# Graph attention and a four-layer end stage: written places for each bank job and reader, the clamp on VectorE, and an end stage issued in written order

## The chip, the core and the metric

The kernel runs on one core of a Trainium2 chip. The metric is the device time in microseconds (us) of one execution. A core has TensorE (matmuls; PE in the profile, its weight loads PEld), VectorE (DVE), ScalarE (ACT), GpSimd (POOL) and SyncE (SP, which here issues most DMAs). TensorE writes to PSUM, which has eight banks; all other tiles lie in SBUF. A matmul of 32-bit floats appears as two matmul instructions in the trace.

## What is computed

Four graph layers follow each other; x has 16 batches of 1024 nodes with 128 features, adj is a sparse 1024 x 1024 matrix per batch.

```python
x = _layernorm(x + L0(x, adj))            # attention
x = _layernorm(x + L1(x, adj, nodemask))  # neighbours thinned out one row after the other, three SAGE layers with batch norm
x = _layernorm(x + L2(x, adj))
x = _layernorm(x + L3(x, adj))

def L0(h, adjacency):
    h_self = h @ W_self_w + W_self_b; h_nb = h @ W_nb_w + W_nb_b
    pre = (h_self @ A1_i)[:, :, None, :] + (h_nb @ A1_j)[:, None, :, :] + A1_b
    scores = (relu(pre) @ A2_w)[..., 0] + A2_b[0]
    attn = softmax(where(adjacency == 0, -1e9, scores))
    return relu(h_self + attn @ h_nb)

def L2(x, adj):
    return relu(adj @ (x @ W + b) + x)

def L3(H, A):
    A1 = A + eye; d = rsqrt(sum(A1, -1))
    return (A1 * d[:, :, None] * d[:, None, :]) @ H @ B
```

## The kernel before

The kernel has one stage after the other. The change touches two of them: the attention (`phase_att`, layer 0) and the end stage (`phase_end`, the last product of layer 1 with its layernorm, then layers 2 and 3).

**Attention.** Since adj is sparse, scores are computed for edges, not for pairs of nodes. The nodes of a batch are cut into 10 groups of 104. A pair of groups (i, j) with j >= i is a unit; a unit holds up to 128 edges, one per partition. Eleven units form a block (`band(r)`), five blocks a batch, so that a batch has 55 units, called slots in the order of the work, and the stage 880. For each unit, `gather` (L516, L521) multiplies the one-hot tables of the edges' ends with the projected features, into one of three PSUM banks `pg`; `score` (VectorE, L533) and `weigh` (ScalarE, L543 and L545) make the weights `hg`; `scatter` (L554) adds the weighted features into three PSUM banks `pa` that hold the batch's sums. The scatter of a unit follows three slots later.

The one-hot tables of a block are made while earlier blocks run, in small jobs on TensorE: `counts` and `offsets` (number the edges of each unit, L351, L362), `beyond` on GpSimd (L374 subtracts, L378 clamps to 0..1; tile `g`, one buffer), `steps` (L411, the difference of clamped rows gives the one-hot table `oh_b` of one end), `ranks` (L383, L389, tile `qs`), `others` (L427; VectorE L435 compares) and `numbers` (L447); `widen` (ScalarE, L441) makes 32-bit copies `oh`, `numbered` (VectorE, L501) the table `we` for the scatter, `one_way` (VectorE, L403) a test for edges without their counterpart. Each job takes one of two PSUM banks `pw` and is followed by its readers on ScalarE or VectorE. The projection of a group of the next batch (`projection`, L303, L306) takes such a bank too; three readers on ScalarE (L315 to L317) and three instructions on VectorE (L318 to L321) follow. Of the batch before, `collect` (L565) takes the sums out of `pa`, `clear` (L264) zeroes them, `end_group` (L598 to L79) finishes a group and its statistics, `end_norm` (L619) the layernorm, `end_turn` (L635, L639) transposes. The mask rows of a later batch are loaded by SP and converted by GpSimd (L280, L282).

The loop `for at in range(B * SLOTS)` writes all of this slot by slot: the gather, then the matmuls of the slot's jobs, the score, the readers of the jobs, the weights, the scatter. `block_job` decides the job of a slot: `steps` in slots 0 to 2 of a block, `others` in 3 to 5, projections in 6 and 7, `ranks` with `counts`, `offsets` and `numbers` in 8 to 10. `as_traced` chains the instructions of each engine, so that every engine runs them in the order in which they are written.

**End stage.** For each batch b, `layer2` and `layer3` run eight iterations each: `neighbours` (L1647, 8 products of adj with `vals` or `v`), then on VectorE the residual sum and the statistics of the rows (`stats`, L78, L79). After iterations 3 and 7, `root` raises the variances of four row tiles to -1/2 on GpSimd (L1586, L1587); `apply` (VectorE, L1591) normalizes them, `turn` transposes them (L1619; ScalarE copies, L1620), `values_2` and `values_3` make the next layer's values (L1626). In between, the next batch's `products_1` (L1603), `rows_1` (the sum with x, L1608, its statistics and the root) and `bias_1` (GpSimd, L1575) are written. `store_slots` issues two indirect DMAs from GpSimd (L1521) that put rows of batch b + 4 into `x1_d`; it is done for b up to 11. `negative` (ScalarE, L1706) tests adj. There is no `as_traced` here: the order on each engine is chosen by the framework's scheduler from priorities and its own estimates.

## Time and profile before

| | |
|---|---|
| Median of 3 runs | 3051.52 us (3046.65 to 3052.65) |
| Profiled execution | 3058.9 us, of which the span from the first to the last instruction is 3056.8 |
| Mean granted TensorE clock | 0.937 |
| Attention stage | from the first score at 59 us to about 1600 us |
| End stage, first product of layer 2 to the end | 2359.75 to 3056.8 us |

The profile is of one execution, taken by the hardware profiler. Durations of matmuls are modelled at their ends, so that TensorE's busy time is not its peak. "Idle before" and the waits are inferred from semaphores. In the views of windows a row has the window, its length, then the busy time of PE, PEld, DVE, ACT and POOL (with the number of instructions), then the mean granted TensorE clock, the share of the DMA engines and GB/s. In the view of waits a row has the waiting instruction, the one that it waits for, the sum in us, the number of waits and the longest. In the timeline and in the chain of waits, the first two numbers are start and length in us.

### The profile page before, as it was taken

The numbers are of one execution on the slowest core, as the hardware profiler recorded it, in microseconds if no ns is written. First come the engines' busy times: TensorE is split into PE (matmuls) and PEld (weight loads), VectorE is DVE, ScalarE is ACT, GpSimd is POOL, SyncE is SP. The second block draws the span as 40 slices with busy tenths as digits, with TensorE's granted clock in tenths as the row PEclk, the third lists the DMA queues.
The fourth block names the chain that finished last, engine by engine and source line by source line (L and its number), as shares of the span: only waits on it lengthen the run. The fifth ranks groups of instructions, "written<-read, shape, count | busy, mean of one in ns | idle before, by whom it ended". The sixth has DMA issues, their size and how long they took to land.

```text
span 3056.8 us, 70983 instructions
## 1 busy us (share of the span) xinstructions
PE 2723.7 (89%) x25724; PEld 2392.3 (78%) x25724; DVE 2191.9 (72%) x8416; ACT 1860.8 (61%) x5689; POOL 1426.8 (47%) x1545
## 2 busy tenths in 40 slices
PE   5999999999999999999968888578796999999997
PEld 3877777777777777777768887377786999999997
DVE  5788888888888888888863567756664666666664
ACT  3888888888888888888862233255654233343332
POOL 3766665666666666666313331244333333233321
PEclk8999999999999999999987777789997999999999
DMA  5323332233322333223026442054455354445440
GB/s 145 100 73 96 102 95 81 71 99 98 93 79 75 103 98 93 76 73 97 22 58 210 145 150 60 17 178 160 169 193 192 113 181 161 147 146 181 160 152 16
DMA packets 179958, 348.60 MB, mean 114 GB/s; under 512 B 14148, under 2 KB 89942, under 8 KB 179472
## 3 DMA queue, kind: packets, MB, share of 16 engines
q1 hardware_dynamic: 173584, 328.15, 33.7%
q0 software_dynamic: 4864, 11.63, 1.3%
q10 hardware_dynamic: 1152, 4.19, 0.5%
q8 instruction: 206, 3.38, 0.5%
q14 instruction: 152, 1.25, 0.1%
HBM read 257.87 MB, written 87.03 MB: 113 GB/s over the span
## 4 chain that ended last, share of the span: by engine, by line
PE 46%; DVE 28%; ACT 9%; issue 7%; DMA 6%; POOL 3%; SPq 0%; POOLq 0%; ACTq 0%; DVEq 0%
PE pg L1647 10%; PE pa L554 5%; DVE junk L533 5%; PE pg L516 4%; PE pg L521 3%; PE pq L1357 3%; DVE we L501 2%; DMA x_d<-keep_xs,keep_row 2%; ACT hg L545 2%; DVE oh_b L435 2%; DVE one_way L403 2%; PE pg L1007 2%; ACT oh L441 2%; DVE st L78 2%; DVE x_rows L601 2%
## 5 line engine op out<-in xcount | busy, mean ns | idle before, releaser
L545 ACT ACTIVATE hg<-pg,hg 128x128 f32<-128x128 f32 x1600 | 510.2, 365 | 28.6
L554 PE MATMUL pa<-hg,we 128*104 128x129 f32 (+1 forms) x3520 | 526.1, 272 | 0.0
L516 PE MATMUL pg<-parts,oh 104*128 104x384 f32 (+1 forms) x1760 | 512.8, 373 | 3.5 <-ACT hg L545 3.3
L554 PEld LDWEIGHTS pa<-hg,we 128*104 128x104 f32 x3520 | 447.7, 171 | 46.5 <-issue 38.2
L533 DVE SCALAR_TENSOR_TENSOR junk<-pg,w_a 128x128 bf16<-128x128 f32 x1600 | 396.7, 281 | 110.9 <-PE pg L521 104.4
L280 POOL TENSOR_SCALAR mask<-ld 104x1024 f16<-104x1024 f32 (+1 forms) x150 | 426.5, 2843 | 39.6 <-DMA ld<-in_adjT 39.4
L521 PE MATMUL pg<-parts,oh 104*128 104x384 f32 (+1 forms) x1760 | 434.3, 328 | 0.0
L374 POOL TENSOR_TENSOR g<-k_next,off 105x512 f16<-105x512 f16 (+1 forms) x240 | 236.4, 985 | 366.4 <-PE pw L411 360.9
L521 PEld LDWEIGHTS pg<-parts,oh 104*128 104x128 f32 x1760 | 311.4, 189 | 0.0
L543 ACT ACTIVATE hg<-sc 128x2 f32<-128x2 f32 (+1 forms) x880 | 187.8, 213 | 160.8 <-DVE junk L533 147.4
L516 PEld LDWEIGHTS pg<-parts,oh 104*128 104x128 f32 x1760 | 268.8, 191 | 21.5 <-ACT oh L441 15.1
L501 DVE TENSOR_TENSOR we<-k_id,ids 128x832 f32<-128x832 f16 (+1 forms) x240 | 259.2, 1080 | 9.3 <-PE pa L554 8.7
L1587 POOL TENSOR_TENSOR rstd<-ve,mhalf 128x4 f32<-128x4 f32 x96 | 97.0, 1011 | 323.9 <-DVE ve L1586 323.8
L441 ACT CAST oh<-oh_b 104x1024 fp32r<-104x1024 bf16 (+1 forms) x240 | 233.4, 973 | 1.0 <-DVE oh_b L435 1.0
L378 POOL TENSOR_SCALAR g<-g 105x512 f16<-105x512 f16 (+1 forms) x240 | 188.7, 786 | 20.7
L303 PE MATMUL pw<-w_all,xT 128*104 128x512 f32 x320 | 172.1, 620 | 24.7 <-ACT x1T L639 9.4
L318 DVE TENSOR_TENSOR parts<-pw,parts 104x384 fp32r<-104x384 f32 x160 | 88.9, 556 | 123.2 <-ACT own L317 122.0
L1591 DVE TENSOR_SCALAR x<-x,mv,rstd 128x128 f32<-128x128 f32 x256 | 104.7, 450 | 91.2 <-POOL rstd L1587 91.2
L435 DVE TENSOR_TENSOR oh_b<-pw,k_slot_edge 104x512 bf16<-104x512 f32 (+1 forms) x240 | 152.6, 636 | 5.6 <-PE pw L427 5.6
L1696 ACT ACTIVATE y<-x,shift,rstd 128x128 f32<-128x128 f32 x128 | 52.7, 482 | 162.9 <-POOL shift L1689 162.9
L403 DVE SCALAR_TENSOR_TENSOR one_way<-qs,mask 104x1040 bf16<-104x1040 f16 (+9 forms) x160 | 146.7, 917 | 1.1 <-ACT qs L396 1.1
L420 ACT CAST oh_b<-pw 104x512 bf16<-104x512 f32 (+1 forms) x240 | 131.2, 547 | 20.4 <-PE pw L411 20.0
(349 smaller groups left out, 6522.1 us busy)
## 6 DMA issues: line engine op xcount, KB each, us to landing
ld<-in_adjT SPq DMA_DIRECT2D x135, 416.0 KB
m<-mask_d SPq DMA_DIRECT2D x16, 2048.0 KB
keep_adj<-in_adjT SPq DMA_DIRECT2D x8, 4096.0 KB
adj<-in_adjT SPq DMA_DIRECT2D x8, 4096.0 KB
mask_d<-mask SPq DMA_DIRECT2D x144, 208.0 KB
hT_d<-uT SPq DMA_DIRECT2D x48, 512.0 KB
h<-hT_d SPq DMA_DIRECT2D x48, 512.0 KB
hT<-hT_d SPq DMA_DIRECT2D x32, 512.0 KB
```

The costliest lines, as they stand in the source:

```text
L280: engine.tensor_scalar(mt[:n, s, :N], ld[:n], 0.0, None, op0=ALU.is_gt)
L374: nc.gpsimd.tensor_tensor(g, k_next[:E].unsqueeze(1).to_broadcast([E, m, C]), v.off[:, n0 : n0 + m].unsqueeze(2).to_broadcast([E, m, C]), ...
L403: nc.vector.scalar_tensor_tensor(junk[:W, :nb, :], v.q[:W, at : at + nb, :W], EDGE, v.mt[:W, i, i * W : NP].rearrange("p (n w) -> p n w", ...
L435: nc.vector.tensor_tensor(v.o[:W, n0 : n0 + m, 1, :], pw[:W, : m * C].rearrange("p (n c) -> p n c", c=C), k_slot_edge[:W].unsqueeze(1).to_ ...
L441: nc.scalar.copy(v.ends[:W, n0 : n0 + m], v.o[:W, n0 : n0 + m])
L501: nc.vector.tensor_tensor(we[:, :n, :], k_id.unsqueeze(1).to_broadcast([P, n, W]), V[b * BANDS + r].ids[:, 2 * lo : 2 * hi].unsqueeze(2).t ...
L516: nc.tensor.matmul(flat[:, first : 3 * F], own, d.parts[i][:W, p, first:], start=p == 0, stop=False, skip_group_check=True,)
L521: nc.tensor.matmul(pg[:, 1::step, :], other, reversed_parts(d.parts[j][:W, p, :], step), start=False, stop=p == 1, skip_group_check=True,)
L533: nc.vector.scalar_tensor_tensor(junk, pg[:, 1 + e, :], 0.0, w_a2, op0=ALU.max, op1=ALU.mult, accum_out=d.sc[:, at + e : at + e + 1],)
L545: nc.scalar.activation(hg[:, e, :F], pg[:, 3 - 3 * e, :], AF.Copy, scale=hg[:, e, F : F + 1])
L554: nc.tensor.matmul(PA[bank][:W, at : at + part.stop - part.start], we[:, 2 * (u - lo) + e, :], hg[:, e, part], start=False, stop=True, ski ...
L1647: nc.tensor.matmul(pg[:, :cols], ADJ[b % 2][:, jt, it * P : (it + 1) * P], v[:, jt, :cols], start=jt == 0, stop=jt == T - 1,)
```

## The change

In attention the slot loop and `block_job` go. Every step gets a written place, a number of slots and a fraction, and all steps are issued in the order of these places: `BANKS` has the place of each bank job within a block, `READ` that of each of its readers, `PROJECT` those of the two projections of a block (the products, then each of the six readers), and so on. The readers of a projection become single steps. The clamp of `beyond` moves from GpSimd to VectorE (`clamp`) and has its own places. The first three blocks' tables, written out by hand before, come from the same table, ahead of slot 0. The masks of batch 1 come every two slots instead of every three; those of later batches get places of their own (`MASKS`).

In the end stage `rows_1` is split into the sum (`add_1`) and the statistics (`stats_1`), with a PSUM tile for each half; transposes and the sum over neighbours run over their parts in reversed order; several steps change places, the two indirect stores among them (from layer 2 to iterations 3 and 5 of layer 3); and `as_traced` fixes the written order on each engine.

The diff, cut:

```diff
+BANKS = (
+    (-2.05, (("step", 0),)), (-0.7, (("step", 1),)), (1.5, (("step", 2),)), (2.05, (("other", 0),)),
+    (3.1, (("other", 1),)), (4.42, (("rank", 1),)), (5.5, (("rank", 0), ("count", 0),)), (5.58, (("other", 2),)),
+    (6.38, (("rank", 2), ("number", 0), ("offset", 0),)),
+)
+READ = {
+    ("step", 0): -1.5, ("step", 1): 0.05, ("step", 2): 1.85, ("rank", 0): 5.82, ("count", 0): 5.75, ("other", 0): 2.5,
+    ("other", 1): 4.36, ("other", 2): 5.9, ("rank", 1): 4.9, ("rank", 2): 7.05, ("offset", 0): 8.31,
+    ("number", 0): 7.56,
+}
+PROJECT = (
+    (6.25, 6.42, 6.54, 7.25, 7.33, 6.85, 16.48), (9.85, 9.9, 10.6, 9.95, 11.38, 11.56, 17.53),
+)
+BEYOND = (3.72, 5.65, 6.42)
+CLAMP = (6.38, 8.56, 11.15)
+NUMBERED = (1.38, 5.32, 9.9)
+ONE_WAY = (-2.25, 5.95)
+WIDEN = (3.38, 6.02, 8.53)
+SCORE, WEIGH, SCATTER = 0.55, 1.01, 0.8
+COLLECT = (3.51, 3.52, 5.3)
+CLEAR = (7.38, 5.9, 6.25)
...
+END_GROUP = (6.58, 9.33, 16.31, 13.9, 28.75, 29.9, 20.38, 27.32, 17.78, 25.5)
+MASKS = (-85.1, -82.25, -66.44, -55.48, -52.46, -49.25, -45.47, -42.18, -35.52, -29.18)
+AHEAD = {"step": 1, "other": 1, "number": 1, "rank": 2, "count": 3, "offset": 3}
+PAUSE = (3, 4, 5, 6)
+BEHIND = 3
...
+        def high():
             hi = d.parts[s] = lp.tile([P, 2, 3 * F], F32R, name=f"parts{s}", bufs=1 if s < 4 else 2)
-            z = sm.tile([P, F], F32, name="z_self", bufs=2)
-            nc.scalar.copy(hi[:W, 0, :], pw[:W, : 3 * F])
-            nc.scalar.copy(z[:W], pw[:W, 2 * F : 3 * F])
-            nc.scalar.copy(d.own[:W, s, :, :F], pw[:W].rearrange("p (a f) -> p a f", f=F)[:, ::3, :])
-            nc.vector.tensor_tensor(hi[:W, 1, :], pw[:W, : 3 * F], hi[:W, 0, :], ALU.subtract)
-            nc.vector.tensor_tensor(z[:W], pw[:W, F : 2 * F], z[:W], ALU.add)
+            nc.scalar.copy(hi[:W, 0, :], job.pw[:W, : 3 * F])
+
+        def other_z():
+            job.z = sm.tile([P, F], F32, name="z_self", bufs=2)
+            nc.scalar.copy(job.z[:W], job.pw[:W, 2 * F : 3 * F])
+
+        def own():
+            nc.scalar.copy(d.own[:W, s, :, :F], job.pw[:W].rearrange("p (a f) -> p a f", f=F)[:, ::3, :])
+
...
-        return products, readers
+        return products, high, other_z, own, low, add_z, self_score
 
     def self_weight(b):
 
...
+        nc.gpsimd.tensor_tensor(
+            v.g[:E, n0 : n0 + m, :], k_next[:E].unsqueeze(1).to_broadcast([E, m, C]),
+            v.off[:, n0 : n0 + m].unsqueeze(2).to_broadcast([E, m, C]), ALU.subtract,
+        )
+
+    def clamp(v, n0, m):
+
         g = v.g[:E, n0 : n0 + m, :]
-        nc.gpsimd.tensor_tensor(
-            g, k_next[:E].unsqueeze(1).to_broadcast([E, m, C]),
-            v.off[:, n0 : n0 + m].unsqueeze(2).to_broadcast([E, m, C]), ALU.subtract,
-        )
-        nc.gpsimd.tensor_scalar(g, g, 1.0, 0.0, op0=ALU.min, op1=ALU.max)
+        nc.vector.tensor_scalar(g, g, 1.0, 0.0, op0=ALU.min, op1=ALU.max)
...
+    PARTS = {
+        "step": (steps, copy_steps), "other": (others, copy_others), "rank": (ranks, copy_ranks),
+        "count": (counts, copy_counts), "offset": (offsets, copy_offsets), "number": (numbers, copy_numbers),
+    }
+    TAKES = {"rank": 4 * W, "count": 16, "offset": 16, "number": 32}
+    held = {}
+
+    def bank_products(parts):
+
+        bank = ps_w.tile([P, 512], F32, name="pw")
+        at = 0
+        for kind, k, v in parts:
+            f, g = PARTS[kind]
+            args = pieces()[k] if kind in ("step", "other", "rank") else ()
+            f(v, *args, bank[:, at:])
+            held[kind, k, v.x] = lambda g=g, v=v, args=args, to=bank[:, at:]: g(v, *args, to)
+            at += TAKES.get(kind, 384)
...
+    for x in range(-3, B * BANDS):
+        b, r = divmod(x, BANDS)
+        at = x * UNITS
+        for u in range(UNITS if x >= 0 else 0):
+            do(at + u, 0.2, open_gather, b, r, u)
+            do(at + u, SCORE, take, score, b, r, u)
+            do(at + u, WEIGH, take, weigh, b, r, u)
+            do(at + u, SCATTER, scatters, b, r * UNITS + u)
+        for k in range(3 if x >= 0 else 0):
+            do(at, NUMBERED[k], numbered, b, r, *CHUNKS[k])
+        for key, parts in BANKS:
+            parts = [(kind, k, x + AHEAD[kind]) for kind, k in parts if 0 <= x + AHEAD[kind] < B * BANDS]
+            if parts:
+                do(at, key, lambda parts: bank_products([(kind, k, block(y)) for kind, k, y in parts]), parts)
+                for kind, k, y in parts:
+                    do(at, READ[kind, k], lambda *key: held.pop(key)(), kind, k, y)
+        for k in range(3):
+            if 0 <= x + 2 < B * BANDS:
+                do(at, BEYOND[k], lambda y, k: beyond(block(y), *pieces()[k]), x + 2, k)
+                do(at, CLAMP[k], lambda y, k: clamp(block(y), *pieces()[k]), x + 2, k)
+            if 0 <= x + 1 < B * BANDS:
+                do(at, WIDEN[k], lambda y, k: widen(block(y), *pieces()[k]), x + 1, k)
+        for k in range(2):
+            if 0 <= x + 1 < B * BANDS:
+                do(at, ONE_WAY[k], lambda y, k: one_way(block(y), k), x + 1, k)
+            if 0 <= x and b + 1 < B:
+                s = ORDER[2 * r + k]
+                do(at, PROJECT[k][0], make, b + 1, s)
+                for i, key in enumerate(PROJECT[k][1:]):
+                    do(at, key, step, b + 1, s)
+    for b in range(B - 1):
+        at = (b + 1) * SLOTS
+        do(at - SLOTS, 2.0, begin, b + 1)
+        do(at - SLOTS, 8.0, empty, b + 1)
+        do(at, 12.75, self_weight, b + 1)
         for s in range(NG):
...
+            key = MASKS[s] if b else 2 * s - SLOTS + 0.05
+            do(at, key - 3 if b else max(key - 3, -SLOTS), load_rows, b + 1, s)
+            do(at, key, mask_step, b + 1, s)
+            do(at, key + 3, mask_store, b + 1, s)
...
+    first = None
+    for key, _, f, args in sorted(todo, key=lambda t: t[:2]):
+        if first is None and key >= 0:
+            first = len(nc.cur_bb.bb.instructions)
+        f(*args)
     as_traced(tc, first)
     b = B - 1
...
     def products_1(b, half, its):
         s = S[b]
+        if half == 0 and its[0] == 0:
+            s.pp = {}
         if its[0] == 0:
-            s.pp = ps_p.tile([P, 4, F], F32, name="pp")
+            s.pp[half] = ps_p.tile([P, 4, F], F32, name="pp")
         for j in its:
             at = slice((half * 4 + j) * P, (half * 4 + j + 1) * P)
             for l in range(3):
-                nc.tensor.matmul(s.pp[:, j, :], s.h[l][:, at], keep.wl[:, l, :], start=l == 0, stop=l == 2)
-
-    def rows_1(b, half):
+                nc.tensor.matmul(s.pp[half][:, j, :], s.h[l][:, at], keep.wl[:, l, :], start=l == 0, stop=l == 2)
+
+    def add_1(b, half):
         s = S[b]
         x = s.x[:, HALVES[half], :]
-        nc.vector.tensor_tensor(x, x, s.pp, ALU.add)
+        nc.vector.tensor_tensor(x, x, s.pp[half], ALU.add)
+
+    def stats_1(b, half):
+        s = S[b]
         for j in range(4):
             stats(s, half * 4 + j)
         root(s, half)
...
         pt = ps_t.tile([P, 4, P], F32, name="pt")
-        for j in range(4):
+        for j in reversed(range(4)):
             nc.tensor.transpose(pt[:, j, :], s.x[:, half * 4 + j, :], c.ident)
         nc.scalar.copy(s.xT[:, half * 512 : half * 512 + 512], pt.rearrange("p t i -> p (t i)"))
 
...
     def neighbours(b, it, v, cols):
         pg = ps_g.tile([P, F + 1], F32, name="pg")
-        for jt in range(T):
+        for jt in reversed(range(T)):
             nc.tensor.matmul(
                 pg[:, :cols], ADJ[b % 2][:, jt, it * P : (it + 1) * P], v[:, jt, :cols],
-                start=jt == 0, stop=jt == T - 1,
+                start=jt == T - 1, stop=jt == 0,
             )
         return pg
 
...
+    first = len(nc.cur_bb.bb.instructions)
     bias_1(0)
     for half in range(2):
         products_1(0, half, range(4))
-        rows_1(0, half)
+    for half in range(2):
+        add_1(0, half)
+        stats_1(0, half)
         apply(S[0], half)
     load(1)
     load_adj(1)
...
                 store(b - 1, 1)
             if more and it == 4:
                 bias_1(b + 1)
-            if it == 5 and b + 4 < B:
-                with tc.issue_after(S[b].first.ins):
-                    store_slots(nc, x1_d, keep, b + 4)
+            if it == 5:
+                apply(S[b], 0)
         turn(b, 0)
         if more:
             products_1(b + 1, 0, range(4))
-            rows_1(b + 1, 0)
-        values_3(b, 0)
+            add_1(b + 1, 0)
         apply(S[b], 1)
         if more:
             products_1(b + 1, 1, range(2))
         turn(b, 1)
+        for half in range(2):
+            values_3(b, half)
         if more:
             products_1(b + 1, 1, range(2, 4))
-        values_3(b, 1)
+            stats_1(b + 1, 0)
+            add_1(b + 1, 1)
         for it in range(T):
             layer3(b, it)
             if more:
                 if it == 0:
-                    rows_1(b + 1, 1)
                     apply(S[b + 1], 0)
+                if it == 1:
+                    stats_1(b + 1, 1)
                 if it == 2:
-                    apply(S[b + 1], 1)
                     turn(b + 1, 0)
                 if it == 3:
-                    turn(b + 1, 1)
+                    apply(S[b + 1], 1)
                 if it == 4:
                     values_2(b + 1, 0)
                 if it == 5:
+                    turn(b + 1, 1)
+                    store(b, 0)
+                if it == 6:
                     values_2(b + 1, 1)
-                    store(b, 0)
                 negative(b + 1, it)
+            if it in (3, 5) and b + 4 < B:
+                store_slots(nc, x1_d, keep, b + 4, (it - 3) // 2)
         if not more:
             store(b, 0)
             store(b, 1)
         if b + 2 < B:
             load(b + 2)
             load_adj(b + 2)
+    as_traced(tc, first)
```

## The prediction

> **What bounds the kernel now.** I read the page first, then the busy time by block of one batch, then TensorE's waits over the attention stage, then the last stage batch by batch. The page's engine row says which engine leads:
>
> ```profile
> PE 2723.7 (89%) x25724; PEld 2392.3 (78%) x25724; DVE 2191.9 (72%) x8416; ACT 1860.8 (61%) x5689; POOL 1426.8 (47%) x1545
> ```
>
> TensorE leads, so a saving counts only where TensorE stands idle or runs slowly. The edits touch two stages: attention (about 59 to 1600 us) and the end stage (about 2320 to 3057). The windows view of attention's batch 7, cut at the starts of its five blocks of eleven slots (length first, then busy time by engine):
>
> ```profile
> 728.12:748.41 20.29, 18.81 (x162) 15.48 (x161) 18.98 (x83) 15.54 (x51) 17.75 (x17) 1.00 0.44 127
> 748.41:767.18 18.77, 17.99 (x159) 14.82 (x158) 17.95 (x77) 15.31 (x50) 11.63 (x10) 1.00 0.23 64
> 767.18:785.97 18.79, 18.07 (x162) 15.02 (x160) 16.57 (x74) 15.60 (x53) 8.16 (x10) 1.00 0.12 37
> 785.97:804.50 18.53, 17.57 (x157) 14.50 (x156) 13.43 (x58) 17.79 (x58) 14.56 (x11) 1.00 0.20 56
> 804.50:823.98 19.48, 18.81 (x168) 15.62 (x168) 13.02 (x58) 16.68 (x55) 9.32 (x11) 1.00 0.59 162
> ```
>
> TensorE is idle for 0.7 to 1.5 us in each block and 4.6 in the batch (95.86 less 91.25), at full clock. VectorE (third busy figure) is nearly as full in blocks 0 to 2: 53.50 of 57.85 us, a slack of 4.35; blocks 3 and 4 leave it 11.6. The view of TensorE's waits from 160 to 1570 us names the idle time:
>
> ```profile
> PE pw L383 <- DVE z_self L319: 33.7, 42, 1.0
> PE pa L264 <- DVE own L565: 14.5, 16, 1.3
> PE pw L303 <- ACT x1T L639: 9.4, 14, 0.7
> PE pw L427 <- DVE oh_b L435: 4.1, 14, 0.3
> PE pg L516 <- ACT hg L545: 3.3, 5, 1.1
> PE pw L303 <- DVE oh_b L435: 3.3, 14, 0.2
> ```
>
> L383 and L303 wait for one of the two `pw` banks, that is for the readers of the job two before: 33.7 + 9.4 + 3.3 = 46.4 us. The other three (21.9) wait for the collected sums, for `oh_b` and for `hg`. Now the end stage: the windows of batch 10, which issues the indirect stores of a later batch, and of batch 13, which issues none:
>
> ```profile
> 2796.71:2840.60 43.89, 41.91 (x354) 40.98 (x353) 28.19 (x114) 16.45 (x36) 13.50 (x15) 0.96 0.45 158
> 2925.04:2965.11 40.07, 39.96 (x354) 39.51 (x353) 26.39 (x114) 16.24 (x36) 11.39 (x13) 1.00 0.38 132
> ```
>
> The same 354 matmuls take 3.8 us longer in batch 10: 2.0 of idle TensorE, and the rest at a mean clock of 0.96 instead of 1.00. The chain of waits inside batch 10 has the reason (start, length, what):
>
> ```profile
> 2806.75 5.92 DMA x_d<-keep_xs,keep_row
> 2812.93 0.97 POOL x_d L1521
> 2813.91 1.05 POOL d L1673
> 2814.97 0.99 POOL rstd L1587
> 2815.98 2.38 DVE x L1591
> 2818.41 1.24 PE pt L1619 x4
> 2819.65 2.56 PE pp L1603 x12
> ```
>
> GpSimd issues one indirect store (L1521), stands until it has landed to issue the second, and only then computes layer 2's `d` and `rstd`, for which `apply`, the transposes and TensorE wait. The 12 products after the wait take 2.56 us; in batch 13 they take 1.34. The four `apply` instructions take 2.38 instead of 1.11, because a GpSimd instruction runs beside them, as the timeline of batch 3 shows:
>
> ```profile
> 2510.56 2.33 POOL L1575 TENSOR_TENSOR x<-x,keep_bl 128x1024 f32<-128x1024 f32 x1
> 2510.62 3.13 DVE L1591 TENSOR_SCALAR x<-x,mv,rstd 128x128 f32<-128x128 f32 x4 [3.27 <-POOL rstd L1587]
> ```
>
> One L1591 has a median of 0.341 and a longest of 2.38 us.
>
> **The change, step by step.** The sum is made against the profiled execution, 3058.9 us (span 3056.8, 2.1 around it). It lies 7.4 above the median of the runs, 3051.5, and I carry the difference over unchanged.
>
> *Bank jobs and readers.* The old loop opens one bank job per slot and reads it in the same slot; the two projections (slots 6 and 7), each with three ScalarE and three VectorE readers, stand right before `ranks`. The table spaces them: projections at 6.25 and 9.85, self scores ten and nearly eight slots later, and by the written positions each bank's last reader stands 0.4 to 2 slots (a slot is 1.74 us) ahead of its next user. I take the whole 46.4 us as gone and the other 21.9 as staying; the two collects now stand together before the clears, which moves that wait but does not shorten the VectorE work in it. Weights, scores and scatters keep their number and, to a fraction of a slot, their places: nothing. The masks of batch 1 come two slots apart instead of three; GpSimd needs 2.77 + 0.38 us for one of the 3.5 that two slots last: nothing. `empty`'s two memsets come six slots later: nothing. Were this cover gone, each would cost its own length, under 3 us once.
>
> *The clamp.* 240 instructions leave GpSimd (L378, 0.786 us mean, off the path: GpSimd waits 360.9 us for the table's readers anyway) and join VectorE, 15 per batch. Before has no float16 `tensor_scalar` of this size on VectorE. From below: its mask row of the prologue, 1024 elements in 0.69 us, so 0.35 for 512; and less than nothing is possible, since VectorE's two-input rows also grow beside GpSimd (L501 from 0.80 to 1.89 us) and meet fewer GpSimd instructions now. From above: a clamp stands behind a whole mask row of GpSimd (2.77), as L1591 stood behind L1575, so 3.1. Queued behind it are the scores, for which ScalarE's weights and then the next gather's bank wait. GpSimd stays busy for 61.4 - 11.8 = 49.6 of about 93 us; in written order a block's three subtractions come before or between its clamps, so mostly masks can be met. I take 0.6, nearer to the lower end: 0.35 and 0.25 of standing. In blocks 3 and 4 the slack hides it (6 x 0.6 of 11.6 us). In blocks 0 to 2 it is 9 x 0.6 = 5.4 against 4.35: 1.05 us per batch, 16 in 15 batches. The Trainium skill ("SBUF — State Buffer", Who interferes with whom) speaks against this edit: a VectorE `tensor_scalar` in a two-port mode and a GpSimd instruction exclude each other for the whole instruction. The L1591 row agrees; by the rule alone, with each of the nine clamps meeting a mask half way, the phase would lose 11.4 us a batch instead of 1.05.
>
> Attention: 46.4 - 16 = 30 us less. In the prologue three clamps (0.61, 0.61, 0.51) leave GpSimd's chain before the first gather, and 0.35 follows the last: 1.4 less.
>
> *End.* The stores go from layer 2 to iterations 3 and 5 of layer 3. There the second still waits for the landing of the first (5.9), and behind it on GpSimd stands layer 3's second `root`; four iterations of 1.79 = 7.2 us and ScalarE's final store, which waits up to 7.9 for `shift` today, hide it. Without that cover the next `rstd` would be late by up to 1. SP's loads now follow the written order; `adj` lands in 14.2 us and is read about 22 later: nothing. The new order's own wait, counted from layer 2's last product with batch 13's lengths: transposes 0.44, 24 products 2.68, 12 products 1.34, so TensorE is through at 4.46. VectorE adds the next batch's first half only after the 24 products (3.12 + 0.7), and the four `apply` (1.11) stand behind that addition: 4.96. So 0.5 us idle instead of 0.1, and about 40.5 per batch. Batches 0 to 11 last 524.7 now, 43.73 each: 12 x 3.23 = 38.8 less. Batches 12 to 14 (120.8): 0.7 more. Batch 15 has no products to fill with and now needs both halves of `v` before layer 3: eight products (0.9), four copies (1.1) and about 1 of slower clock, 3 more. Net 35 less. The Trainium skill ("TensorE: Matmul & The Clock Gate", Why this matters for your kernels) has the clock fall only after gaps of some 3 us; here waits of 2.0 on average (22.3 us in 11, the longest 2.9) went with 0.96. By the page End would give 12 x 2.0 = 24 before those two costs.
>
> Sum: 30 + 1.4 + 35 = 67; 3058.9 - 67 = 2992 for a profiled execution, **2984 us** for the median.
>
> **Rivals.**
> (a) *VectorE becomes the bound through the clamps.* Place: blocks 0 to 2 of each batch. Price: 9c - 4.35 us per batch for a clamp of c. All other gains are 46.4 + 1.4 + 35 = 83, or 5.5 per batch, so it is slower from c = 1.1. With c = 1.75 (0.35 and half a mask row) it is 171 - 83 = 88 more: 3140. For it: L1591's 2.38. Against: the ten masks hold GpSimd for 28 of some 93 us of a batch, so that by chance three clamps in ten meet one, and six of the fifteen stand where VectorE has room.
> (b) *The bank waits return under other names*, since the same readers run on the same two busy engines. Attention gives nothing: 3015.
> (c) *The end stage's wait only changes its name*: if the addition or `rstd` comes 1 us later than counted, the gap is 1.5 and the clock falls as in batch 10. At 43 per batch End gives 8.8 - 3.7 = 5: 3015. Against it: the 24 products give `rstd` (2.5 after the last product) room.
> (d) *All idle time of attention goes and the clamps are hidden*: 68.3 + 1.4 + 35 = 105 less, 2947.
>
> **Numbers.** Forecast 0.5, (a) 0.11, (b) or (c) 0.25, (d) 0.14. A measurement of this kernel can tell about 0.2% (6 us) from no change. Only (a) ends on the other side: slower 0.11, within 0.02, faster 0.87. The range takes in (d) below, with 3 us for End's terms, and above it (b) and (c) with 15 us for a clamp of up to 0.7: 2944 to 3030. (a) and the tails are what it leaves out.
>
> **What would show it.** Right: no wait of L383 and L303 for bank readers; attention's batches near 93.5 us; VectorE over 0.95 in blocks 0 to 2; the clamp's median below 0.4 with a tail; the end stage's first twelve batches near 40.5 at clock 1.00. Wrong: a clamp mean over 1.1 us, new gather waits for `hg` or scores, or an end batch still over 43.

## The result, and the profile after

The changed kernel takes 3009.4 us (median, 3002.2 to 3013.4), the kernel before 3049.1 in the same comparison (3045.0 to 3052.7): a ratio of 0.9868, 95% interval 0.9844 to 0.9891, or 40 us less (33 to 48). I had forecast 67 less. The profiled execution took 3010.3 us with a span of 3008.3, against 3058.9 and 3056.8 before, 48.6 less; stage by stage in the two traces:

| stage | before, us | after, us | difference | forecast |
|---|---|---|---|---|
| up to the first gather | 57.1 | 57.9 | +0.8 | -1.4 |
| attention, first gather to last scatter | 1522.6 | 1506.9 | -15.7 | -30 |
| the stages between, same code | 780.0 | 772.0 | -8.0 | 0 |
| end stage, first `pg<-vals` to the end | 697.1 | 671.4 | -25.7 | -35 |

The 8 us of the middle are not the change's: in the executions of this study that stage lasts from 768 to 787 us with the same code. Attention brought half of what I wrote down for it, the end stage three quarters.

The engine row of the page of after, columns as before:

```profile
PE 2685.3 (89%) x25724; PEld 2410.0 (80%) x25724; DVE 2251.2 (75%) x8656; ACT 1841.1 (61%) x5689; POOL 1256.7 (42%) x1305
```

The 240 clamps are there: VectorE has 240 instructions more (8416 before), GpSimd 240 fewer. The view of the clamp's line:

```profile
L428 DVE TENSOR_SCALAR g<-g x240: 245/288/1122, 50.2 to 1535.1; 105x512 f16<-105x512 f16 x80, 105x384 f16<-105x384 f16 x40
```

The median of 0.288 us lies below the 0.6 that I took, and so does the mean, 81.7 us for 240 or 0.34; the longest is 1.12. Now the windows of attention's batch 7, block by block (length, then PE, PEld, DVE, ACT, POOL, clock):

```profile
720.11:739.70 19.59, 18.74 (x162) 15.75 (x161) 18.94 (x86) 15.31 (x52) 12.65 (x12) 1.00 0.57 156
739.70:758.11 18.41, 17.47 (x160) 15.21 (x158) 17.77 (x77) 14.65 (x49) 12.57 (x10) 1.00 0.35 94
758.11:778.96 20.85, 19.25 (x162) 16.86 (x160) 19.14 (x83) 15.45 (x51) 12.53 (x11) 0.92 0.23 68
778.96:796.34 17.38, 17.26 (x158) 15.07 (x156) 12.77 (x58) 17.05 (x57) 6.19 (x5) 1.00 0.01 1
796.34:815.61 19.27, 18.51 (x169) 16.02 (x168) 13.14 (x64) 17.03 (x57) 6.22 (x5) 1.00 0.42 119
```

Blocks 0, 1, 3 and 4 are shorter than before. Block 2, 18.79 before, is 20.85 now, and its mean clock is 0.92. That is so in seven of the batches 1 to 14 (20.5 to 20.9 us): one stretch of 3.41 us at half the clock falls in each. In the other seven block 2 lasts 19.2 to 19.6 us at full clock, as in batch 6:

```profile
664.11:683.35 19.24, 17.65 (x161) 15.38 (x160) 18.76 (x81) 15.22 (x51) 11.67 (x9) 1.00 0.25 73
```

A stretch costs about 1.6 us, and attention has seven of them (23.9 us at half clock), where it had two before (6.8). TensorE's waits in attention (160 to 1570 us):

```profile
PE pw L433 <- DVE oh_b L485: 42.8, 52, 1.7
PE pw L461 <- DVE z_self L364: 19.4, 28, 0.8
PE pw L497 <- DVE oh_b L485: 1.3, 3, 0.5
PE pg L551 <- ACT hg L580: 0.7, 2, 0.4
```

The waits before were 68.3 us; these and the 0.3 of one more line are 64.5. No projection waits for a bank any longer, and the collects' 14.5 are gone. In their place the ranks jobs (L433) wait 42.8 us for the reader of an others job (L485), and the steps (L461) for a projection's `z_self`. This is rival (b) of the prediction: the bank waits came back under other names. Cut by slot of the batch, with the mean of batches 1 to 14, the trace has 2.8 us a batch of it at one place: slot 6 of blocks 0, 1 and 2 (0.43, 0.81 and 1.57), where the third ranks job follows the third others job.

So TensorE's idle time did not shrink: over batches 1 to 14 it is 64.7 us before and 64.9 after. What shrank is its busy time (with the ends of matmuls modelled), from 1280.3 to 1270.1 us, in spite of the slower clock. The products of steps and of others add 4.9 us a batch to it instead of 6.6 (each counted up to the start of the next product), although one of them lasts about as long as before (medians of 0.376 and 0.217 us, before 0.391 and 0.219). That these jobs overlap their neighbours better was no term of the forecast, and no run takes it apart.

The end stage, windows of batch 7, which issues indirect stores, and of batch 13, which issues none:

```profile
2624.40:2665.48 41.08, 40.01 (x354) 39.44 (x353) 29.37 (x114) 16.57 (x37) 13.39 (x15) 1.00 0.47 169
2871.27:2912.37 41.10, 40.02 (x355) 39.45 (x354) 29.39 (x114) 16.59 (x37) 11.35 (x13) 1.00 0.46 167
```

The two are alike now and at full clock, 41.1 where I had worked out 40.5. The timeline of batch 7 shows the 1.07 us of idle TensorE as two gaps:

```profile
2635.25 2.35 POOL L1605 TENSOR_TENSOR x<-x,keep_bl 128x1024 f32<-128x1024 f32 x1
2635.65 2.10 DVE L1699 SCALAR_TENSOR_TENSOR x<-o,x 128x128 f32<-128x128 f32 x1
2638.20 1.08 DVE L1621 TENSOR_SCALAR x<-x,mv,rstd 128x128 f32<-128x128 f32 x4
2639.34 0.66 PE L1654 MATMUL pt<-ident,x 128*128 128x128 f32 x4 [0.49 <-DVE x L1621]
...
2642.79 0.69 DVE L1640 TENSOR_TENSOR x<-x,pp 128x512 f32<-128x512 f32 x1 [1.18 <-POOL rstd L1617]
2643.39 1.11 DVE L1621 TENSOR_SCALAR x<-x,mv,rstd 128x128 f32<-128x128 f32 x4
2644.56 0.66 PE L1654 MATMUL pt<-ident,x 128*128 128x128 f32 x4 [0.54 <-DVE x L1621]
```

The second gap is the one I had counted: `apply` (L1621) stands behind the addition (L1640). The first I had not: `bias_1` on GpSimd (L1605) makes one VectorE instruction of 0.29 us take 2.10, and the first `apply` comes late. Before, the first twelve batches had nine stretches of 3.41 us at half clock, at 1.7 us or less some 15 of the 31 us that they gained; now they have none.

### The profile page after: what moved, and what is told of

It is laid out like the page before. It is cut to its first block, busy times and chain, and to the rows that moved or that the text cites. A ratio compares the mean times of both kernels' runs of the same rounds, so it can differ in the third digit from the quotient of the medians.

```text
span 3008.3 us, 71053 instructions
## 1 busy us (share of the span) xinstructions
PE 2685.3 (89%) x25724; PEld 2410.0 (80%) x25724; DVE 2251.2 (75%) x8656; ACT 1841.1 (61%) x5689; POOL 1256.7 (42%) x1305
## 5 line engine op out<-in xcount | busy, mean ns | idle before, releaser
L551 PE MATMUL pg<-parts,oh 104*128 104x384 f32 (+1 forms) x1760 | 521.5, 378 | 0.9 <-ACT hg L580 0.7
L589 PE MATMUL pa<-hg,we 128*104 128x129 f32 (+1 forms) x3520 | 518.0, 271 | 0.3 <-DVE we L536 0.3
L589 PEld LDWEIGHTS pa<-hg,we 128*104 128x104 f32 x3520 | 466.5, 172 | 9.6 <-DVE we L536 0.5
L556 PE MATMUL pg<-parts,oh 104*128 104x384 f32 (+1 forms) x1760 | 439.1, 331 | 0.0
L420 POOL TENSOR_TENSOR g<-k_next,off 105x512 f16<-105x512 f16 (+1 forms) x240 | 241.9, 1026 | 314.6 <-PE pw L461 293.9
L556 PEld LDWEIGHTS pg<-parts,oh 104*128 104x128 f32 x1760 | 314.4, 191 | 0.1
L551 PEld LDWEIGHTS pg<-parts,oh 104*128 104x128 f32 x1760 | 276.7, 192 | 27.7 <-issue 13.9
L1655 ACT COPY xT<-pt 128x512 f32<-128x512 f32 x64 | 37.5, 586 | 376.1 <-PE pt L1654 343.6
L536 DVE TENSOR_TENSOR we<-k_id,ids 128x832 f32<-128x832 f16 (+1 forms) x240 | 255.0, 1063 | 0.0
L485 DVE TENSOR_TENSOR oh_b<-pw,k_slot_edge 104x512 bf16<-104x512 f32 (+1 forms) x240 | 154.0, 642 | 16.1 <-PE pw L477 15.5
L1461 DVE BATCH_NORM_STATS2 stats<-pt 128x6 f32<-128x512 f32 x120 | 79.5, 692 | 70.3 <-PE pt L1457 69.2
L568 DVE DVE_READ_ACCUMULATOR junk<-pg,w_a 128x1 f32 x1600 | 132.0, 82 | 0.0
L453 DVE SCALAR_TENSOR_TENSOR one_way<-qs,mask 104x1040 bf16<-104x1040 f16 (+9 forms) x160 | 126.3, 789 | 1.5 <-ACT qs L446 1.5
```

The source lines that it names most:

```text
L420: nc.gpsimd.tensor_tensor(v.g[:E, n0 : n0 + m, :], k_next[:E].unsqueeze(1).to_broadcast([E, m, C]), v.off[:, n0 : n0 + m].unsqueeze(2).to_ ...
L485: nc.vector.tensor_tensor(v.o[:W, n0 : n0 + m, 1, :], pw[:W, : m * C].rearrange("p (n c) -> p n c", c=C), k_slot_edge[:W].unsqueeze(1).to_ ...
L536: nc.vector.tensor_tensor(we[:, :n, :], k_id.unsqueeze(1).to_broadcast([P, n, W]), V[b * BANDS + r].ids[:, 2 * lo : 2 * hi].unsqueeze(2).t ...
L551: nc.tensor.matmul(flat[:, first : 3 * F], own, d.parts[i][:W, p, first:], start=p == 0, stop=False, skip_group_check=True,)
L556: nc.tensor.matmul(pg[:, 1::step, :], other, reversed_parts(d.parts[j][:W, p, :], step), start=False, stop=p == 1, skip_group_check=True,)
L568: nc.vector.scalar_tensor_tensor(junk, pg[:, 1 + e, :], 0.0, w_a2, op0=ALU.max, op1=ALU.mult, accum_out=d.sc[:, at + e : at + e + 1],)
```

## The experiments

All comparisons are against the kernel before on the same chip; differences in us are the ratio's, taken of 3048. The chips differ by more than some of these effects (the kernel before had medians of 3045 to 3059), so the runs are set side by side by ratio. Attention's length is from each run's trace.

**The two parts apart.** `att_only` has the attention of after and the end stage of before, `end_only` the reverse.

```
att_only:  phase_end, store_slots of before in the changed file
end_only:  phase_end, store_slots of after in the file before
```

> The changed attention with the end stage of before. Theory (the attention table gives little because its waits only change their names, VectorE being full in blocks 0 to 2): about 15 us less than before, 3034, with the end stage's first twelve batches back at 43.7 and clock 0.96. Rival (attention did give the 30 us of the prediction, and the middle stages or the end stage lost some): 30 us less, 3020.

> The attention of before with the changed end stage. Theory (the end stage gives all that its period says, 12 x 2.6 less 3 for batch 15, and is independent of attention): about 26 us less than before, 3023, periods of 41.1. Rival (the two parts help each other, for instance through the clock): clearly less than 26, and the two single gains do not add up to 40.

`att_only` measured 0.9969 (0.9957 to 0.9981), 9 us less; its attention lasts 1509.5 us and the end stage's first twelve batches 44.3 on average. `end_only` measured 0.9925 (0.9912 to 0.9938), 23 us less, with periods of 41.1. Together 32, with 40 from the whole: within the intervals they add up. The 9 us of attention are less than even the theory's 15. The shortfall against the forecast is then 16 to 22 us in attention with its prologue and 9 to 12 in the end stage (by the stages of the traces, and by these two runs).

**The stores put back.** In the changed kernel:

```diff
+            if it == 5 and b + 4 < B:
+                store_slots(nc, x1_d, keep, b + 4)
             if it == 5:
                 apply(S[b], 0)
...
-            if it in (3, 5) and b + 4 < B:
-                store_slots(nc, x1_d, keep, b + 4, (it - 3) // 2)
```

> The changed kernel with both indirect stores of a batch in layer 2 at iteration 5 again, before apply; all else in the new written order. Theory (the place of the stores made the gap and lowered the clock): the first twelve batches of the end stage back near 44 us at a clock of about 0.96, 12 x 2.9 = 35 us more than the changed kernel, 3044. Rival (the written order and the two halves of v made the gain): at most 5 us more, 3014.

Measured 0.9981 (0.9970 to 0.9993): 34 us of the 40 are lost again. The first twelve batches last 44.3 on average (41.1 to 46.3), batches 12 to 14, which issue no stores, 41.1 as in the changed kernel. The window of batch 8:

```profile
2695.68:2739.78 44.10, 41.56 (x355) 41.04 (x354) 29.44 (x114) 16.70 (x37) 13.35 (x15) 0.96 0.45 158
```

Idle time (2.5 us) and the slower clock (0.96) are back with the stores, so their place in GpSimd's queue made the end stage's gain, not the written order: with the stores back, the whole end stage lasts 709.7 us, longer than the 697.1 before.

**The end stage's two gaps.** In the changed kernel:

```diff
-            if more and it == 4:
+            if more and it == 0:
                 bias_1(b + 1)
...
-            add_1(b + 1, 0)
         apply(S[b], 1)
         if more:
+            add_1(b + 1, 0)
             products_1(b + 1, 1, range(2))
```

> The changed kernel with two moves in the end stage: bias_1 of the next batch at iteration 0 of layer 2 instead of 4, and the second apply ahead of the addition of the next batch's first half. Theory (the two gaps of 0.5 us a batch are VectorE standing beside bias_1, which makes the first apply late, and the second apply standing behind the addition of 0.7): both gaps go, the period falls from 41.09 to about 40.1, 15 us less, 2994. Rival (the gaps move: the later addition delays the next batch's statistics and its first transposes): the period stays within 0.3 of 41.1, 3005 or more.

Measured 0.9822 (0.9803 to 0.9840), 14 us less than the changed kernel by the ratios. The period is 39.62 in fourteen of the fifteen batches:

```profile
2611.44:2651.06 39.62, 39.58 (x355) 39.39 (x353) 29.05 (x114) 16.57 (x37) 13.29 (x15) 1.00 0.51 175
```

TensorE is idle for 0.04 us. `bias_1` still stretches an instruction (L1699 took 1.80 in iteration 1), but four iterations before anything waits for it. Both gaps are explained; the two moves were not tried one by one. The last batch lasts 57.9 us here and 54.8 in the changed kernel, but that is not these moves: in the runs with the changed kernel's own end stage it lasts from 54.3 to 58.4.

**The clamp back on GpSimd.** My first theory for attention was VectorE's load: blocks 0 to 2 of batch 7 show it 97, 97 and 92% busy. Then work taken from it should pay.

```diff
-CLAMP = (6.38, 8.56, 11.15)
+CLAMP = (3.73, 5.66, 6.43)
...
-        nc.vector.tensor_scalar(g, g, 1.0, 0.0, op0=ALU.min, op1=ALU.max)
+        nc.gpsimd.tensor_scalar(g, g, 1.0, 0.0, op0=ALU.min, op1=ALU.max)
```

> The changed kernel with the fifteen clamps of a batch on GpSimd again, each right behind its subtraction; all else as in the changed kernel. Theory (VectorE's load bounds blocks 0 to 2): VectorE loses nine clamps of 0.28, 2.5 us, in those blocks, ranks and steps wait less for its readers, and attention gives up to 37 us more; I expect about 20, a time near 2990. Rival (the table needs the clamp off GpSimd, whose masks would hold up the steps): no better than the changed kernel, 3009 or more, with new waits of the steps for GpSimd.

A miss: 0.9944 (0.9932 to 0.9956), 23 us slower than the changed kernel instead of 20 faster. Attention lasts 1532.9 us, longer than before the change. All of it is in block 2, which on average lasts 22.0 us (20.1 in the changed kernel), as in its batch 7:

```profile
773.16:794.62 21.46, 19.24 (x162) 16.95 (x160) 19.38 (x76) 15.32 (x51) 15.08 (x14) 0.92 0.22 66
```

VectorE is only 90% busy there, so something other than its load holds it. The wait at slot 6 is 2.2 us in place of 1.57, which makes 9 of the 27 us that block 2 grew by; the rest is the clock, with 68 us at half clock in place of 24.

**Less work on VectorE.**

```diff
             if 0 <= x + 1 < B * BANDS:
-                do(at, ONE_WAY[k], lambda y, k: one_way(block(y), k), x + 1, k)
+                pass
```

> The changed kernel without its test for one-way edges (L453, two VectorE instructions of 0.8 us a block; the flag stays at zero). Theory (load): 5.2 us of VectorE's work leave blocks 0 to 2 of each batch; ranks and steps no longer wait for its readers, the 64.5 us of these waits shrink to under 30, a time near 2975. Rival (the order: a bank's reader stands right ahead of its next user, whatever VectorE's load): waits and time nearly as now, 3000 or more.

Measured 0.9833 (0.9815 to 0.9850), 11 us less than the changed kernel by the ratios; attention 1502.3, 4.6 less. The clock fell in ten batches here, not in seven, so that at the same clock it would have been some 9 (estimated with 1.6 us for each). Block 2 and the waits:

```profile
760.18:780.85 20.67, 19.26 (x161) 16.97 (x160) 17.71 (x76) 15.28 (x50) 12.06 (x11) 0.92 0.23 69
```

```profile
PE pw L433 <- DVE oh_b L485: 42.5, 53, 1.6
PE pw L461 <- DVE z_self L364: 16.5, 22, 0.8
```

VectorE does 1.4 us less in this block, is 86% busy, and block 2 is as long as ever; the ranks wait 42.5 us as against 42.8. Some 80 us of VectorE's work in 14 batches (5.7 a batch) are gone for some 9 in attention. The theory of VectorE's load has fallen. What counts is what stands ahead of one reader, not how much the engine does in all.

**What stands there.** The timeline of the changed kernel in block 2 of batch 7, from slot 4 to the end of the wait:

```profile
764.78 1.04 POOL L420 TENSOR_TENSOR g<-k_next,off 105x512 f16<-105x512 f16 x1
...
764.98 2.72 DVE L536 TENSOR_TENSOR we<-k_id,ids 128x832 f32<-128x832 f16 x1
...
765.79 2.76 POOL L313 TENSOR_SCALAR mask<-ld 104x1024 f16<-104x1024 f32 x1
...
767.63 0.34 DVE L633 SCALAR_TENSOR_TENSOR own<-own,rz 104x128 f32<-104x128 f32 x1
...
769.52 0.55 DVE L485 TENSOR_TENSOR oh_b<-pw,k_slot_edge 104x384 bf16<-104x384 f32 x1
...
770.12 0.29 PE L433 MATMUL pw<-cnt,k_offs 104*128 104x312 f16 x1 [1.60 <-DVE oh_b L485]
```

The others product that L485 reads was done at 766.4; L485 starts at 769.52. Ahead of it in VectorE's queue stand a number table (L536), a group of the batch end (L633 and three more), a self score and two scores. The table begins 0.2 us after a GpSimd subtraction with two inputs; a mask row follows on GpSimd, and the table takes 2.72 us (median 1.015). In block 2 of batches 1 to 13 the trace has 2.72 or 2.73 each time: not chance but the table of places. After the wait of 1.6 us the block's mean clock is 0.92, and TensorE's busy time is 19.25 where it is 17.65 in batch 6, which has the same wait (1.59) and keeps its clock.

Two causes are on offer now: the meeting with GpSimd, and the order ahead of L485. First the mask row alone:

```diff
-MASKS = (-85.1, -82.25, -66.44, -55.48, -52.46, -49.25, -45.47, -42.18, -35.52, -29.18)
+MASKS = (-85.1, -82.25, -66.44, -61.0, -55.48, -52.46, -49.25, -45.47, -42.18, -35.52)
```

> The changed kernel with one number of its table moved: the last mask row of the next batch no longer starts at slot 25.8 (block 2, right behind a subtraction of GpSimd) but the ten rows take nine of their old places and one in block 4 (slot 49). Theory (what lengthens block 2 is one meeting: the number table of L536, two inputs on VectorE, stands behind GpSimd's subtraction and the start of this mask row and takes 2.72 us instead of 0.84 in all 14 batches): L536 back near 0.9 in block 2, block 2 from 20.1 to about 18.9, attention about 17 us less, 2992. Rival (VectorE's load alone bounds blocks 0 to 2): the load is the same, block 2 stays near 20, 3009.

Measured 0.9857 (0.9841 to 0.9872), which does not stand apart from the changed kernel's 0.9868 by the times. The trace does show that the meeting is gone: the longest L536 of all is 1.66 us, L433's waits fall from 42.8 to 32.0, and block 2 shrinks from 20.1 to 19.3 on average. Batch 7:

```profile
757.50:777.11 19.61, 18.15 (x162) 15.45 (x160) 19.17 (x84) 15.42 (x51) 9.43 (x7) 1.00 0.17 45
```

The clock is 1.00 in all batches, with waits at slot 6 that now stay near 1.0 (0.95 on average). Attention is 6.5 us shorter, not 17: blocks 0, 3 and 4 grew by 0.1 to 0.2 each, and the order ahead of L485 still costs its 0.95. And the gain of block 2, 0.77 a batch or 11 us, is that of the seven stretches at half clock: beside the changed kernel's seven batches at full clock (19.35 on average) it is hardly shorter. What was won at slot 6, 0.6 us, was for the most part lost again in the same block (its slot 0 takes 1.61 us on average instead of 1.14). So what this move saved was the clock.

Then the order alone:

```diff
-NUMBERED = (1.38, 5.32, 9.9)
+NUMBERED = (1.38, 6.0, 9.9)
...
-END_GROUP = (6.58, 9.33, 16.31, 13.9, 28.75, 29.9, 20.38, 27.32, 17.78, 25.5)
+END_GROUP = (6.58, 9.33, 14.7, 13.9, 28.75, 29.9, 20.38, 26.45, 17.78, 25.5)
```

> The changed kernel with three numbers of its table moved: the second number table (L536) from slot 5.32 to 6.0, behind the reader of the third others job (slot 5.9), and the two groups of the batch end that stand at slot 5.3 of blocks 1 and 2 to slots 3.7 and 4.45 of the same blocks. VectorE's work in each block stays the same. Theory (order: the third ranks job, slot 6.38, takes the bank of the third others job, whose only reader stands on VectorE behind a table, a group and two scores, 3 us of work in a slot of 1.7): the waits of L433 at slot 6, 2.8 us a batch in blocks 0 to 2, fall under 1.0; attention about 25 us less, 2984. Rival (VectorE's load in blocks 0 to 2): no change, 3009. Second rival (the meeting with GpSimd's mask row goes over to the reader or the table at its new place): half of it, 2997.

Slower than the changed kernel by 20 us: 0.9934 (0.9922 to 0.9946), attention 1518.6. In block 1, where no mask row stands near slot 4, the order did what it should: the wait at slot 6 fell from 0.81 to 0.1. In block 2 the second rival came true, and worse than priced. The timeline of batch 7:

```profile
771.39 2.41 DVE L633 SCALAR_TENSOR_TENSOR own<-own,rz 104x128 f32<-104x128 f32 x1
771.61 1.04 POOL L420 TENSOR_TENSOR g<-k_next,off 105x512 f16<-105x512 f16 x1
772.62 2.76 POOL L313 TENSOR_SCALAR mask<-ld 104x1024 f16<-104x1024 f32 x1
...
775.10 0.21 ACT L578 ACTIVATE hg<-sc 128x2 f32<-128x2 f32 x1 [2.93 <-DVE junk L568]
...
775.62 0.55 DVE L485 TENSOR_TENSOR oh_b<-pw,k_slot_edge 104x384 bf16<-104x384 f32 x1
...
776.22 1.62 PE L340 MATMUL pw<-w_all,xT 128*104 128x512 f32 x2 [1.84 <-DVE oh_b L485]
```

Now the group that I had moved ahead meets the same pair of GpSimd instructions, takes 2.41 us in place of 0.34, and the wait of 1.84 has moved on to the projection. The view names L485; but by the order of the table the projection takes the bank of the ranks job at place 5.5, whose readers on ScalarE (L405, L446) start at 775.85 and 775.90, behind weights that had waited 2.93 us for a score on VectorE. Block 2 grew by 1.05 a batch: 0.25 of wait, and the rest the clock, with 47.8 us at half clock in nine batches.

**Groups moved to the emptier blocks.** By the windows VectorE has 4.6 and 6.1 us of room in blocks 3 and 4.

```diff
-END_GROUP = (6.58, 9.33, 16.31, 13.9, 28.75, 29.9, 20.38, 27.32, 17.78, 25.5)
+END_GROUP = (6.58, 9.33, 16.31, 13.9, 28.0, 29.5, 34.5, 37.5, 40.9, 44.05)
...
-        do(at, END_ROOT, end_root, b)
+        do(at, END_ROOT, end_root, b, 4, NG)
+        do(at, 45.3, end_root, b, 0, 4)
... (rows 0 to 3: norms at 47.2 to 49.0, store at 50.0, their turn last)
```

> The changed kernel with the last four groups of the batch end (rows 0 to 3) moved from blocks 1 and 2 (slots 17.8 to 27.3) to blocks 3 and 4 (34.5 to 44), with their own root, norms, store and turn behind them. Theory (load): each group is four VectorE instructions, 1.0 to 1.3 us; two leave each of blocks 1 and 2, where VectorE is 96% full; block 2 from 20.1 to about 18.8, block 1 by 0.3, about 20 us less, 2989. Rival (order or the one meeting with the mask): under 5 us. Against both: block 3, where ScalarE is 98% full, may grow by up to 1 us a batch, 15 us more.

A miss: 0.9978 (0.9967 to 0.9989), 34 us slower than the changed kernel. Blocks 1 and 2 became 0.6 and 0.7 shorter on average, block 3 2.3 longer and block 4 1.0. Blocks 3 and 4 of batch 7:

```profile
791.51:811.29 19.78, 17.86 (x157) 15.03 (x156) 16.95 (x70) 16.59 (x55) 6.29 (x5) 1.00 0.05 12
811.29:831.51 20.22, 18.77 (x170) 16.13 (x168) 14.38 (x68) 17.97 (x59) 7.46 (x8) 1.00 0.36 101
```

The waits of ScalarE and of TensorE over attention:

```profile
ACT own L357 <- DVE x_rows L636: 23.5, 14, 1.8
```

```profile
PE pg L551 <- ACT hg L580: 17.8, 14, 1.3
```

Once a batch ScalarE's copy into `own` now stands 1.7 us behind a group's instruction on VectorE, and once a batch a gather stands 1.3 behind ScalarE's `hg`; in the changed kernel that second wait was 0.7 us in all. VectorE's free time there was no room for bursts. Which of the moved rows costs how much was not taken apart.

**All that helped, together**, and two variants of it.

```diff
 end_order, reader_first, and:
-MASKS = (-85.1, -82.25, -66.44, -55.48, -52.46, ..., -35.52, -29.18)
+MASKS = (-85.1, -82.25, -72.0, -66.44, -55.48, -52.46, ..., -35.52)
-END_NORM = (..., 43.54, 42.75, 42.53)       END_STORE = 45.1
+END_NORM = (..., 44.9, 46.9, 47.9)          END_STORE = 48.5
-        do(at, DIVIDE, end_seen, b)
+        do(at, 7.6, end_seen, b)
```

> The changed kernel with all that helped, put together: the end stage's two moves; the three numbers of reader_first; the mask row of slot 25.8 moved to slot 38, in block 3; three norms of ScalarE and the store of the rows moved from block 3 to block 4 (slots 44.9 to 48.5), so that a projection's readers are not queued behind them; end_seen behind the projection's readers. Theory (order): the end stage's period 39.6 (22 less, less 3 in the last batch), attention 25 less from the reader, 8 from the mask row, up to 10 from block 4's step and block 0's: 2950. Rival (load): the end stage's 19 and the mask row's 7 alone: 2983.

Measured 0.9713 (0.9701 to 0.9726): 87 us less than before and 47 less than the changed kernel; on the scale of the expectations (3009 for the changed kernel) that is 2962, between the two. The end stage is 19.0 shorter than there (652.4). Attention lasts 1473.7, 33 less. Its batch 7:

```profile
707.64:726.59 18.95, 18.68 (x163) 15.78 (x161) 18.40 (x83) 14.80 (x49) 13.09 (x12) 1.00 0.54 150
726.59:745.88 19.29, 18.52 (x160) 15.36 (x158) 18.79 (x81) 15.15 (x51) 13.09 (x10) 1.00 0.35 99
745.88:764.17 18.29, 17.79 (x162) 15.37 (x160) 17.71 (x82) 15.24 (x51) 8.72 (x7) 1.00 0.26 69
764.17:781.55 17.38, 17.26 (x157) 15.08 (x156) 13.29 (x58) 16.69 (x56) 10.18 (x10) 1.00 0.10 26
781.55:800.44 18.89, 18.55 (x169) 16.00 (x168) 13.61 (x62) 17.27 (x57) 7.18 (x5) 1.00 0.39 113
```

92.8 us where the prediction had 93.5. TensorE is idle for 2.0 us of it at full clock, and VectorE is still 97% busy in blocks 0 to 2: that figure was never the bound. No stretch at half clock falls in batches 1 to 14, and TensorE's idle time there is 31.9 us instead of 64.9.

Then the clamp's engine, and the order, each in this kernel without the meeting:

```diff
 combined_clamp:  the two edits of clamp_pool
 combined_order:  NUMBERED and END_GROUP as in the changed kernel
```

> The combined kernel with the fifteen clamps of a batch on GpSimd again, each right behind its subtraction. Theory (what the clamp on GpSimd cost in clamp_pool, 22 us, belonged to block 2 and its mask row): with the mask row gone from there the clamp's engine matters little, within 8 us of the combined kernel's 2973. Rival (the clamp on VectorE is a gain by itself, because a subtraction and a clamp in a row on GpSimd hold up two-input instructions of VectorE wherever they stand): 15 us or more above it, 2988 or more.

> The combined kernel with the second number table and the two groups at their old slots again, ahead of the reader of the third others job. Theory (the meeting with the mask row was all; the order ahead of the reader matters little once it is gone): within 8 us of 2973. Rival (both count, and reader_first lost only because the meeting went over to one of the moved groups): the waits of L433 at slot 6 come back with about 1.5 us a batch in blocks 1 and 2, 15 to 20 us above the combined kernel, 2990.

`combined_clamp` measured 0.9713 (0.9694 to 0.9733), the same as `combined`; its attention is 3.3 us longer. So the 23 us that a clamp on GpSimd cost in `clamp_pool` belonged to block 2 as it stands in the changed kernel; by itself the engine of the clamp is worth nothing that can be measured here. That the mask row made it so is likely and not shown alone, since `combined` also has the other order. `combined_order` measured 0.9734 (0.9714 to 0.9755), 6 us above `combined` with overlapping intervals; its attention is 12.3 longer and L433's waits are back with 28.9 us, 0.35, 0.47 and 0.95 a batch in blocks 0 to 2. That lies between the two expectations: of the 33 us that `combined` takes off attention, the order ahead of L485 has about 12; the mask row, the norms and `end_seen` together have the other 21. Some 11 of these 21 are the seven stretches at half clock, which `combined_order` does not have either.

## Why the prediction was right, and where its terms were off

The sign and the two places of the gain were right, its size was not. In the end stage the mechanism was right too. In attention it was not: the idle time that was to go is still there, and that attention became shorter all the same, by 9 to 16 us through a shorter busy time that the forecast did not have, was luck. By the steps of the prediction:

- **Bank jobs: 46.4 us gone.** This step failed, and with it the forecast of attention. I read the places of the table as times: "each bank's last reader stands 0.4 to 2 slots ahead of its next user". But VectorE runs its instructions in the written order. At slot 5.9 of blocks 0 to 2 the reader of the third others job stands behind some 3 us of work, and in block 2 behind a meeting with GpSimd that adds another 1.7 to 1.9. The old waits went, as I said; 62 us of new ones came, of which I had none in the sum, and seven stretches at half clock, some 11 us, that I had not priced either. Of my signs, the batches near 93.5 us did not come (95.4 on average), and L433 waits. Rival (b), at a quarter of the chances with (c), had described it, with nothing for attention: it gave 9 us in `att_only`, 16 in the trace.
- **The other 21.9 staying.** They did not stay: the collects' wait is gone, and `oh_b` (now for the numbers) and `hg` make 2.0 us. This was an error in the other direction.
- **The clamp, 9 x 0.6 - 4.35.** The size was wrong (mean 0.34; 3.3 us per batch in blocks 0 to 2, not 5.4), and the formula was too: it took VectorE's slack in blocks 0 to 2 as the price's threshold. `no_one_way` gave slack back and got little for it. Rival (a) needed a clamp of over 1.1 us and rests on the same reading. In this kernel the move of the clamp saves 23 us all the same, because without it GpSimd's longer chain meets more of VectorE's instructions in block 2 (in batch 7 L536 takes 2.05 us, L633 0.69 and L636 1.01, by themselves 1.0, 0.34 and 0.29) and the clock falls more often; `combined_clamp` shows that this gain belongs to the other places of the table, and not to the clamp's engine.
- **The masks.** Here was much of the cost. I wrote "nothing" for the rows of batch 1, had no term for the new places of the later ones, and weighed their meetings only with clamps, three in ten by chance. The table makes the meetings certain, once a batch at the same instruction, and it was not the clamp but the number table that was met. The section of the Trainium skill that I had weighed against the clamp ("SBUF — State Buffer", Who interferes with whom) also has a VectorE instruction with two SBUF inputs contend with a GpSimd instruction that reads SBUF, and calls it an exclusive lock. That is the case of L536 in these rows, 2.72 us instead of 1.0. Where they differ is the mask row: L536 ended at 767.70, while the row ran on to 768.55, so it did not hold VectorE for its whole 2.76 us.
- **End, 40.5 a batch.** The mechanism is shown by `stores_back` (34 of the 40 us). The term was off by 0.6: the gap behind the addition is 0.54 as counted (its sum, 3.12 + 0.7 + 1.11, is 4.93 and not 4.96), and `bias_1` makes a second one of 0.49 that I had left out, though I had quoted its row. Twelve batches gained 31.4 instead of 38.8, batches 12 to 14 lost 2.5 instead of 0.7; batch 15 is 3.2 longer against a forecast of 3, which is luck: with the same end stage it lasts 54.3 to 58.4 us in the other runs, 2.7 to 6.9 more than before.
- **Clock.** The end stage's clock returns to 1.00 with two gaps of 0.5 us a batch, and rival (c) did not come true. The rule that only gaps of some 3 us cost clock (the Trainium skill, "TensorE: Matmul & The Clock Gate", Why this matters for your kernels) does not hold here: in the changed kernel waits of 1.2 to 1.6 us went with 0.92 in seven batches, and the measurement decides.
- **The prologue** gave nothing that can be read: the first gather starts 0.8 later, not 1.4 earlier, and with the same prologue from 56.1 to 59.0 in the other runs.

What stays open: what made TensorE's busy time in attention shorter; in which batches a wait costs the clock; why `mask_moved` alone gave only 6.5 us of attention (its moved rows met other instructions, by up to 0.9 us a batch at the clamps of block 1 and 0.8 at the self scores of block 4, but these were not tried one by one); and what the moved norms and `end_seen` give by themselves in `combined`.

## What to carry to other kernels

A table of places fixes which instructions of two engines meet. So price a reader by what stands ahead of it in its own engine's queue, not by its distance in the table, and look for the one meeting that returns in every round. An engine that is 97% busy is not the bound until work taken from it makes the stage shorter: here 5.7 us less a batch on VectorE gave 4.6 us in all of attention (some 9 at the same clock), while moving one mask row and a handful of places, at the same load, gave 33. And look at the clock of every round before a difference is put down to a wait: the same wait of 1.6 us cost 1.6 us more in one batch and nothing more in another. The place where an engine has room on average is no place for a burst, if a short chain (score, weight, next gather) runs through it.

## What the runs showed of the hardware

- What a GpSimd instruction holds up differs. `bias_1` (two inputs, L1605) held a two-input VectorE instruction nearly until its end: L1699, 0.29 by itself, started 0.40 after `bias_1` and ended at 2637.75, 0.15 after it. The subtraction (two inputs, L420) does so too: in batch 14 L536 meets two of them in a row, takes 2.51 us and ends 0.88 after the second. The mask row (one input, float32 to float16, 2.76 us) let go much earlier: L536 ended 0.85 before the row's end. If it stood still until it was let go, then with its own 0.8 to 1.0 it ran from about 766.8, 1.0 us after the row's start. Of the larger tables of the changed kernel (128x832), the 44 that met a mask row alone took up to 1.60 us, the 50 that met one subtraction alone up to 1.11, and the 13 that met one of each 2.72 or 2.73.
- In attention the clock falls to half for stretches of 3.41 us, which cost 1.4 to 1.6 us each, and the length of the wait alone does not say when. In block 2 of the changed kernel waits of 1.57 to 1.60 went with 0.92 in six batches, waits of 1.56 to 1.68 with 1.00 in seven, and one of 1.23 with 0.92. In `reader_first` waits of 1.81 to 1.92 went with 1.00 in five batches, with 0.92 in three and with 0.85 (a stretch of twice that length) in five, and one of 1.62 with 0.92; in `clamp_pool` waits of 2.0 to 2.3 always cost it. At 0.95 to 1.0 at the same place (`mask_moved`) the clock never fell, but before the change it fell twice in block 0, with 1.4 us of idle time in several pieces, the longest 0.87. In the end stage two gaps of 0.5 us a batch left it at 1.00, and 2.5 us of idle time went with 0.96.
